# Groups of 512 nodes, more rows copied by hand and evictions on VectorE in a relational graph convolution

## The chip, the cores and the metric

The kernel runs on one core of a Trainium2 chip. The metric is the device time of one execution in microseconds. TensorE (PE) multiplies matrices, VectorE (DVE) and ScalarE (ACT) work element by element, GpSimd (POOL) issues the gathers here, and SyncE (SP) issues DMAs. ScalarE can issue DMAs as well, and does.

## The reference

Two layers of a relational graph convolution, then a residual and a layer norm. There are 50,000 nodes of 128 features, 850,000 edges sorted by target, 50,000 of them self loops, and 16 relations whose weights are mixtures of 8 bases.

```python
def _rgcn_layer(h, src, dst, rel, basis, w_comp, loop_w, bias):
    W = jnp.einsum('rb,bio->rio', w_comp, basis)
    seg = dst.astype(jnp.int32) * N_REL + rel.astype(jnp.int32)
    agg = jax.ops.segment_sum(h[src], seg, num_segments=N_ENT * N_REL)
    agg = agg.reshape(N_ENT, N_REL, -1)
    msg = jnp.einsum('nri,rio->no', agg, W)
    out = msg + h @ loop_w + bias
    return jax.nn.relu(out)
...
h = _rgcn_layer(entity_emb, src, dst, rel_type, basis1, w_comp1, loop_w1, bias1)
h = _rgcn_layer(h, src, dst, rel_type, basis2, w_comp2, loop_w2, bias2)
...
x = _layernorm(x + _L0_gnn_ref(x, ...), axis=-1)
```

## The kernel before

**Edges.** The first part of the program reads the edge list in ten blocks (`runs`), takes the 50,000 self loops out, and lays the other 800,000 edges out again (`FULL`, read back by `rows_of`). They make 6,250 tiles of 128 edges; ten tiles are a chunk, so a layer has C = 625 chunks. For each edge there is its source (`src`), the place of its target within a window of WN = 12 nodes (`key`) and its relation. This preparation is spread over the first chunks of layer 1, one step of the generator `coming` for each chunk.

**A chunk.** For each of its ten tiles the 128 source rows of 512 bytes are brought into a buffer `g` (L202, one indirect DMA of GpSimd for each tile). PE multiplies the tile with `hot`, which holds for each edge its weight for each of 8 bases, put at one of 12 places (L971): out comes, for one tile, a 128x96 sum in a PSUM tile `pa` that holds five tiles. Two evictions a chunk take `pa` to `aT` (ScalarE, L979). Two chunks later `slots` multiplies `aT` with the 8 bases (L734) into 120 slots, which ScalarE copies to SBUF (L739), and three chunks later `nodes_of` moves the slots to 128 nodes with masks (`masks_of`, L753; the product at L761). The nodes' own part, self loop and bias are added (L764) and the result is stored. In layer 2, the residual and the layer norm come before the store (`normed_steps`).

**The nodes' own part.** `from_itself` takes 128 nodes at a time: a load, a transpose, two products with four bases each (L710), their weighting on VectorE (L713), the loop product and bias (L722, L723), a sum over bases (L726) and a store to a DRAM tensor `L` (L727). `loaded` reads `L` back at the base node of each chunk, an offset that SyncE loads into a register. Neighbouring chunks' windows of 128 nodes overlap.

**Who brings the rows.** GpSimd gathers two chunks ahead (FETCH), into GATHERS = 5 buffers; the first gather of a chunk waits for the last product that read its buffer, by a dependency added by hand. From chunk 9 on, the last tile of every eighth chunk is not gathered: `row_by_row` has SyncE copy its 128 rows by 128 DMAs, each with an offset loaded from DRAM, and ScalarE does so for another of every eight chunks.

```python
HANDS = ((nc.sync, BY_HAND - 1), (nc.scalar, BY_HAND // 2 - 1))
def by_hand(c):
    return BY_HAND < c < C and ks(c) == K and any(c % BY_HAND == at for _, at in HANDS)
```

The DMAs of one such tile are spread over the eight chunks before its use, between the other instructions of their engine. Offsets are loaded 16 at a time (L798) and the rows are issued at L808.

**Order.** PE, GpSimd, VectorE and ScalarE run in the order in which the program states the work; `beside` puts a step of the own part, of `slots` or of the node part behind each of the ten products. All DMAs that SyncE and ScalarE issue take one of eight semaphores in turn, in the program's order, and each waits until the one before it on the same semaphore has landed.

Of the kernel before, what the change touches and what calls it, by code (L numbers as in the profile page):

```python
# [39 lines left out]
F32 = mybir.dt.float32  # L40
I32 = mybir.dt.int32
# [21 lines left out]
AHEAD = 4  # L63
# [8 lines left out]
BASES = 8  # L72
BY_HAND = 8
# [8 lines left out]
def tile_rgcn_resnorm(  # L82
# [21 lines left out]
    NG, NT = -(-R // P), -(-N // P)  # L104
# [9 lines left out]
    assert D == P and N >= P and edges.shape[0] == 1 and AT * NR == P and PER * NB * WN <= BANK and AT * PER * NB == WEIGHTS and PER == HALF and S <= P and C >= 4 and M > 0 and RUN - LK // 2 == LIVE and 2 * C <= NG * P and N <= 1 << 16 and E % ROW == 0  # L114
# [10 lines left out]
    ROW_AT = dram.tile([2 * C, P], I32, name="ROW_AT")  # L125
    NL = -(-(N + LK) // P) * P
    LREL = dram.tile([2 * NL, 1], I32, name="LREL")

    L = [dram.tile([N, D], F32, name=f"L{n}") for n in range(2)]
# [67 lines left out]
    ps_o = ctx.enter_context(tc.tile_pool(name="ps_o", bufs=1, space=PSUM))  # L197
    ps_n = ctx.enter_context(tc.tile_pool(name="ps_n", bufs=1, space=PSUM))
    ps_h = ctx.enter_context(tc.tile_pool(name="ps_h", bufs=2, space=PSUM))
# [6 lines left out]
    def turned(h, m, sb):  # L206

        tp = ps_o.tile([P, D], F32, name="po")
        nc.tensor.transpose(tp[:, :m], h, ident[:m, :m])  # L209
        hT = sb.tile([P, P], F32, name="hT")  # L210
        nc.scalar.copy(hT[:, :m], tp[:, :m])  # L211
        return hT[:, :m]
# [8 lines left out]
    key = consts.tile([P, 2 * C * HALF], BF16, name="key")  # L221


    base_i = consts.tile([1, C], I32, name="base_i")
    slot = consts.tile([P, C], F32, name="slot")
    next_slot = consts.tile([P, C], F32, name="next_slot")
    last_slot = consts.tile([P, 1], F32, name="last_slot")
    first_of = consts.tile([1, C], F32, name="first_of")
    base1 = consts.tile([1, C], F32, name="base1")
    minus = consts.tile([1, S], F32, name="minus")  # L230
# [4 lines left out]
    picked = consts.tile([P, 5 * NG + len(ROWS) + 4], F32, name="picked")  # L235
    ones = consts.tile([P, max(LIVE, C)], F32, name="ones")
# [10 lines left out]
    nc.vector.memset(minus, -1.0)  # L247
# [5 lines left out]
    def set_up(pool):  # L253
# [14 lines left out]
        po = ps_o.tile([P, D], F32, name="po")  # L268
# [146 lines left out]
    def loops_of(g, pool, m, d_i, k_f, r_i, loop, loops, asked):  # L415
# [15 lines left out]

        nc.vector.tensor_scalar(picked[0:1, 5 * g + 4 : 5 * g + 5], d_i[0:1, 0:1], float(asked()), None, op0=OP.is_ge)
        yield
# [8 lines left out]
    def rows_of(j, pool):  # L442
# [3 lines left out]
        parts = pool.tile([P, 2, LIVE, 2], F32, name="parts")  # L446
        for h in range(2):
            nc.sync.dma_start(
                parts[:m, h],
                FULL[h * NP + r0 * LIVE : h * NP + (r0 + m) * LIVE].rearrange("(p e) w -> p e w", e=LIVE),  # L450
            )
        if j:
            yield
        srcf = pool.tile([P, LIVE], F32, name="srcf")
        nc.vector.tensor_tensor(srcf[:m], parts[:m, 0, :, 0], parts[:m, 1, :, 0], op=OP.add)
        node = pool.tile([P, LIVE], I32, name="node")
        nc.vector.tensor_tensor(node[:m], parts[:m, 0, :, 1], parts[:m, 1, :, 1], op=OP.add)
# [20 lines left out]
        row_at = pool.tile([P, LIVE], F32, name="real").bitcast(I32)[:, :P]  # L478
        nc.vector.tensor_scalar(row_at[:m], srcf[:m, LIVE - P :], float(N - 1), float(4 * D), op0=OP.min, op1=OP.mult)
        nc.sync.dma_start(ROW_AT[r0 : r0 + m], row_at[:m])  # L480

# [3 lines left out]
        keyf = pool.tile([P, LIVE], F32, name="keyf")  # L485
# [6 lines left out]
        if (r0 + m) * LIVE > M:  # L492
# [6 lines left out]
                beyond[:m], place[:m, :LIVE], last[:m], 64.0, op0=OP.subtract, op1=OP.mult  # L499
# [8 lines left out]
        po = ps_o.tile([P, D], F32, name="po")  # L508
# [6 lines left out]
        nc.vector.tensor_scalar(base1[:, c0 : c0 + cs], half[0:1, :, 0], float(N - P), None, op0=OP.min)  # L515
        nc.vector.tensor_scalar(base_i[:, c0 : c0 + cs], base1[:, c0 : c0 + cs], float(4 * D), None, op0=OP.mult)

        a, b = max(c0 - 1, 0), c0 + cs - 1
        off = pool.tile([1, P], F32, name="off")
        nc.vector.tensor_tensor(off[:, : b - a], base1[:, a + 1 : b + 1], base1[:, a:b], op=OP.subtract)  # L520
        yield
        po = ps_o.tile([P, D], F32, name="po")
        for h in range(2):
            nc.tensor.matmul(po[:S, :cs], spread[h], half[:, :, h], start=h == 0, stop=False)
        nc.tensor.matmul(po[:S, :cs], minus, base1[:, c0 : c0 + cs], start=False, stop=True)
        nc.vector.tensor_scalar(slot[:S, c0 : c0 + cs], po[:S, :cs], within[:S], None, op0=OP.add)
        yield
        po = ps_o.tile([P, D], F32, name="po")
        nc.tensor.matmul(po[:, : b - a], ones[0:1, :P], off[:, : b - a], start=True, stop=True)
        nc.vector.tensor_tensor(next_slot[:S, a:b], slot[:S, a:b], po[:S, : b - a], op=OP.subtract)  # L530
        if b == C - 1:
            nc.vector.tensor_tensor(
                last_slot[:S], next_slot[:S, b - 2 : b - 1], po[:S, b - a - 1 : b - a], op=OP.subtract
            )
# [6 lines left out]
            ones[:m, :LIVE],  # L541
# [6 lines left out]
    def count_up(pool):  # L548
        last = 5 * NG + len(ROWS)
        off = pool.tile([1, C], F32, name="off_all")  # L550

        nc.vector.memset(off, float(N - 1))
        nc.vector.tensor_copy(off[:, : C - 1], first_of[:, 1:])
        nc.vector.tensor_tensor(off, off, base1, op=OP.subtract)
        nc.vector.scalar_tensor_tensor(
            off, off, float(P - 1), ones[0:1, :C], op0=OP.is_le, op1=OP.mult, accum_out=picked[0:1, last : last + 1]
        )

        in_time = pool.tile([1, C], F32, name="in_time")
        nc.gpsimd.iota(  # L560
            in_time,
            pattern=[[P * NT // C, C]],
            base=P * AHEAD - P,
# [3 lines left out]
        nc.vector.tensor_tensor(off, base1, in_time, op=OP.subtract)  # L567
        nc.vector.scalar_tensor_tensor(
            off, off, 0.0, ones[0:1, :C], op0=OP.is_le, op1=OP.mult, accum_out=picked[0:1, last + 1 : last + 2]
        )  # L570

        nc.vector.tensor_tensor(off[:, : C - 3], base1[:, 2 : C - 1], first_of[:, 1 : C - 2], op=OP.subtract)
        nc.vector.tensor_tensor(off[:, C - 3 : C - 2], base1[:, C - 1 :], first_of[:, C - 3 : C - 2], op=OP.subtract)
        nc.vector.scalar_tensor_tensor(
            off[:, : C - 2],
            off[:, : C - 2],
            1.0,
            ones[0:1, : C - 2],
            op0=OP.is_ge,
            op1=OP.mult,  # L580
            accum_out=picked[0:1, last + 3 : last + 4],
        )
        nc.vector.tensor_scalar(picked[0:1, last + 2 : last + 3], first_of[:, 0:1], 0.0, None, op0=OP.is_equal)
# [3 lines left out]
        total = ps_o.tile([P, D], F32, name="po")  # L587
# [4 lines left out]
            off[:, 1:2], total[:1, 1:2], float(E + 2 * NG * (P + 1) + 3 * C - 1), None, op0=OP.not_equal  # L592
# [3 lines left out]
    def normed(t, m, sb):  # L596

        *_, o = normed_steps(t, m, sb)
        return o

    def normed_steps(t, m, sb):
        st = sb.tile([P, 6], F32, name="st")
        nc.vector.bn_stats(st[:m], t)  # L603
        mv = sb.tile([P, 2], F32, name="mv")
        nc.vector.bn_aggr(mv[:m], st[:m])  # L605
        sd = sb.tile([P, 1], F32, name="sd")
        nc.scalar.activation(sd[:m], mv[:m, 1:2], AF.Sqrt, bias=eps[:m])  # L607
        yield
        rs = sb.tile([P, 1], F32, name="rs")
        nc.vector.reciprocal(rs[:m], sd[:m])  # L610
        nm = sb.tile([P, 1], F32, name="nm")
        nc.vector.scalar_tensor_tensor(nm[:m], mv[:m, 0:1], -1.0, rs[:m], op0=OP.mult, op1=OP.mult)  # L612
        o = sb.tile([P, D], F32, name="o")
        nc.scalar.activation(o[:m], t, AF.Identity, bias=nm[:m], scale=rs[:m])  # L614
        yield o

    def chunked():
        with (
# [8 lines left out]
            def at(c):  # L627

                if c % BASES == 0:
                    _, starts[:] = nc.values_load_multi_w_load_instructions(  # L630
                        base_i[0:1, c : min(C, c + BASES)],
                        engines=[mybir.EngineType.SP],
                        min_val=0,
                        max_val=(N - P) * 4 * D,
                        skip_runtime_bounds_check_because="bases are clamped to N - P, and no node is below 0",
                    )
                return starts[c % BASES]

            def nodes_at(of, start):
                return of.bitcast(U8).rearrange("n d -> (n d)")[ds(start, P * 4 * D)].rearrange("(p d) -> p d", p=P)  # L640

            def weights(c, n):
# [14 lines left out]
                for j in range(PER):  # L657
# [6 lines left out]
                    )  # L664
                yield pm.rearrange("e (t b) -> e t b", b=NB)

            def loop_weights(i, n):

                m = min(AT, NT - i) * NR
                rel = hp.tile([P, 2, P], I32, name="lrel")  # L670
# [544 lines left out]
```

## Time and profile before

| | before |
|---|---|
| median of 10 runs | 15,407.47 us (15,404.69 to 15,415.10) |
| the profiled execution, time | 15,413.04 us |
| its span | 15,411.3 us |
| granted TensorE clock in it | 0.805 |
| busy: PE, DVE, ACT, POOL | 11,650.9, 6,792.2, 2,523.9, 11,586.3 us |
| gathers (L202) | 2 x 6,096 |
| rows copied by hand (L808), each of SyncE and ScalarE | 2 x 9,856 |
| share of the 16 DMA engines, software and hardware queues | 18.7%, 9.0% |

The page gives busy time for each engine, with instructions that only issue a DMA or wait left out, so that SyncE has no line and a queue of DMAs on ScalarE does not count as busy. The groups give for each line the number of instructions, their mean duration in ns and the idle time of the engine just before them with what ended it; "issue" stands for idle time in which nothing was waited for. In a timeline the first column is the start in us, the second the time that the merged instructions took, and what stands in brackets is the idle time before them.

### The profile page before, as it was taken

How to read it: one execution, taken by the hardware profiler on the slowest of the kernel's cores; microseconds unless marked ns; L12 is line 12 of the kernel's file. 1: busy time of each engine (PE TensorE's matmuls, PEld its weight loads, DVE VectorE, ACT ScalarE, POOL GpSimd, SP SyncE). 2: the span in 40 equal slices, each digit the busy share in tenths (PEclk: the TensorE clock that was granted, in tenths of full speed). 3: DMA queues.
4: the chain of work that ended last, by engine and by line, in shares of the span. 5: the costliest groups of instructions: out<-in, count | busy, mean ns of one | idle time of the engine just before them, and what ended most of it. 6: DMA issues, size and time to landing. Idle time of an engine off the chain costs nothing. (4 is left out here: it accounts for less than half of the span.)

```text
span 15411.3 us, 255870 instructions
## 1 busy us (share of the span) xinstructions
PE 11650.9 (76%) x59202; PEld 9222.6 (60%) x59202; DVE 6792.2 (44%) x14585; ACT 2523.9 (16%) x6567; POOL 11586.3 (75%) x12224
## 2 busy tenths in 40 slices
PE   5777777776777777777777777777777777777777
PEld 4656666655565665556566565656666666655556
DVE  6544544445333333333344444444444444444444
ACT  1111111111111111111111111111111111111111
POOL 6777777777777777777777777777777777777777
PEclk8787787777788788888878888787777788788887
DMA  3222222222222222222222222222222222222222
GB/s 95 83 86 86 83 85 85 81 85 80 81 75 75 75 75 75 75 74 75 74 76 80 80 80 80 80 81 80 80 81 80 81 80 80 81 79 81 80 80 75
DMA packets 1236470, 1232.33 MB, mean 80 GB/s; under 512 B 318004, under 2 KB 1028332, under 8 KB 1234940
## 3 DMA queue, kind: packets, MB, share of 16 engines
q0 software_dynamic: 393696, 806.61, 18.7%
q1 hardware_dynamic: 798604, 397.62, 9.0%
q10 hardware_dynamic: 42640, 11.62, 0.3%
q8 instruction: 481, 7.88, 0.2%
q14 instruction: 1049, 8.59, 0.2%
HBM read 1059.71 MB, written 154.87 MB: 79 GB/s over the span
## 5 line engine op out<-in xcount | busy, mean ns | idle before, releaser
L971 PE MATMUL pa<-hot,g 128*128 128x96 f32 x24384 | 5953.0, 337 | 3302.8 <-DMA g<-H,src 1592.5
L971 PEld LDWEIGHTS pa<-hot,g 128*128 128x128 f32 x24384 | 4606.1, 234 | 5681.6 <-DMA g<-H,src 2233.8
L202 POOL DMA_INDIRECT g<-in_x_dram,src x6096 | 5794.4, 951 | 1890.2 <-issue 1764.5
L202 POOL DMA_INDIRECT g<-H,src x6096 | 5766.2, 946 | 1876.6 <-issue 1792.2
L734 PE MATMUL ps<-basis,aT 128*120 128x128 f32 x20000 | 3990.8, 334 | 0.0
L734 PEld LDWEIGHTS ps<-basis,aT 128*120 128x120 f32 x20000 | 3386.2, 237 | 0.0
L979 ACT COPY aT<-pa 128x480 f32<-128x480 f32 x2500 | 1397.9, 559 | 8246.9 <-DMA by_hand<-in_x_dram 3002.0
L713 DVE TENSOR_TENSOR by<-hb,lw 128x512 f32<-128x512 f32 x1564 | 1077.6, 689 | 3697.9 <-PE hb L710 3687.3
L710 PE MATMUL hb<-basis,hT 128*128 128x512 f32 x3128 | 2120.2, 767 | 4.2 <-ACT hT L211 4.2
L726 DVE TENSOR_REDUCE ls<-by 128x128 f32<-128x1152 f32 (+1 forms) x782 | 1657.0, 2119 | 13.5
L871 DVE TENSOR_TENSOR hot<-fixed,own 128x960 f32<-128x960 f32 x1250 | 1446.8, 1157 | 62.5 <-DVE own L864 1.8
L723 DVE TENSOR_TENSOR by<-po,bias 128x128 f32<-128x128 f32 (+1 forms) x782 | 227.6, 291 | 2267.9 <-PE po L722 2236.4
L761 PE MATMUL pn<-slots,own 120*128 120x128 f32 x5000 | 967.0, 325 | 32.9 <-DVE a L764 28.4
L864 DVE TENSOR_TENSOR own<-fixed,key 128x120 f32<-128x120 f32 x1250 | 343.1, 274 | 1139.2 <-PE fixed L658 1136.3
L761 PEld LDWEIGHTS pn<-slots,own 120*128 120x128 f32 x5000 | 813.0, 231 | 36.0 <-DVE a L764 30.5
L710 PEld LDWEIGHTS hb<-basis,hT 128*128 128x128 f32 x3128 | 601.8, 239 | 7.6 <-ACT hT L211 7.6
L607 ACT ACTIVATE sd<-mv,eps 128x1 f32<-128x1 f32 x625 | 184.2, 295 | 2375.6 <-DMA by_hand<-H 1871.7
L658 PE MATMUL fixed<-each,is_rel 128*128 128x64 f32 x3140 | 515.9, 326 | 3.9 <-DVE is_rel L653 3.9
L658 PEld LDWEIGHTS fixed<-each,is_rel 128*128 128x128 f32 x3140 | 497.6, 244 | 4.6 <-DVE is_rel L653 4.3
L209 PE MATMUL po<-ident,h_own 128*128 128x128 f32 (+1 forms) x782 | 271.9, 348 | 278.4 <-ACT lw L689 224.5
L614 ACT ACTIVATE o<-a,nm,rs 128x128 f32<-128x128 f32 x625 | 308.2, 493 | 960.8 <-DMA by_hand<-H 494.2
L753 DVE TENSOR_SCALAR own<-col,slot 120x128 f32<-120x128 f32 x1250 | 422.6, 338 | 0.0
(152 smaller groups left out, 4294.0 us busy)
## 6 DMA issues: line engine op xcount, KB each, us to landing
by_hand<-in_x_dram ACTq DMA_DIRECT2D x9856, 0.5 KB
by_hand<-in_x_dram SPq DMA_DIRECT2D x9856, 0.5 KB
by_hand<-H ACTq DMA_DIRECT2D x9856, 0.5 KB
by_hand<-H SPq DMA_DIRECT2D x9856, 0.5 KB
g<-in_x_dram,src POOLq DMA_INDIRECT x6096
g<-H,src POOLq DMA_INDIRECT x6096
ls_of<-L SPq DMA_DIRECT2D x1250, 64.0 KB
L<-ls SPq DMA_DIRECT2D x780, 64.0 KB
```

What stands on the lines that cost most here:

```text
L202: return nc.gpsimd.indirect_dma_start(out=to, out_offset=None, in_=of, in_offset=bass.IndirectOffsetOnAxis(ap=idx, axis=0))
L658: nc.tensor.matmul(of[:, :, j * NB : (j + 1) * NB], is_rel[:m, j * P : (j + 1) * P], EACH[n][:m], start=True, stop=True,)
L710: nc.tensor.matmul(hb[:m], hT, BASIS[n][:, b : b + few, :].rearrange("p b d -> p (b d)"), start=True, stop=True)
L713: nc.vector.tensor_tensor(by[:m, b : b + few, :], hb[:m].rearrange("p (b d) -> p b d", d=D), lw[:m, b : b + few, None].to_broadcast([m, fe ...
L726: nc.vector.tensor_reduce(ls[:m], by[:m].rearrange("p b d -> p d b"), AX.X, OP.add)
L734: nc.tensor.matmul(ps[: k * WN], aT[:, b, : k * WN], BASIS[n][:, b, :], start=b == 0, stop=b == NB - 1)
L753: nc.vector.tensor_scalar(own[:k], col[:k], at_node[:k], None, op0=OP.is_equal)
L761: nc.tensor.matmul(pn, own, st[i][: ks(i) * WN], start=j == 0, stop=j == len(masks) - 1)
L864: nc.vector.tensor_tensor(own[:, : ks(c)], grid[:, None, :].to_broadcast([P, ks(c), WN]), key[:, c * K : c * K + ks(c), None].to_broadcast ...
L871: nc.vector.tensor_tensor(hot[:, : ks(c)], pm[:, c % Q * K : c % Q * K + ks(c), :, None].to_broadcast([P, ks(c), NB, WN]), own[:, : ks(c), ...
L971: product = nc.tensor.matmul(pa[:, i * NB * WN : (i + 1) * NB * WN], g[:, k + i, :] if k + i < ks(c) - by_hand(c) else handed.pop(c), hot[ ...
L979: nc.scalar.copy(aT[:, :, k * WN : (k + m) * WN].rearrange("d b (i w) -> d i b w", w=WN), pa[:, : m * NB * WN].rearrange("d (i b w) -> d i ...
```

## The change

- Nodes are treated in groups of J x 128 = 512, four nodes to a partition. The 98 groups of a layer are summed in PSUM over all chunks that can touch them (`first(g)` to `final(g)`, 10 or 11 chunks); the slots are spread to four columns by `which` and moved by one product 128x512 for each chunk and group. The loop product is added to the same PSUM tile. `L` in DRAM, its store and its reading back at an offset are gone; the own part stays in SBUF. The nodes' result, norm and store go by 512.
- The evictions of `pa` go from ScalarE to VectorE; the copy of the slots becomes a VectorE product with `which`.
- SyncE and ScalarE copy a tile in every fifth chunk each, from chunk 6 on, spread over five chunks; offsets are loaded 32 at a time.
- The dependency by hand is gone: each gather waits for the product that read its own tile of the buffer.
- PSUM: one bank for `slots`, two for the groups' sums, two shared by the transposes and the own part.

```diff
-BASES = 8
-BY_HAND = 8
+J = 4
+NEAR = 128
+SP_EVERY = 5
+ACT_EVERY = 5
+OFFSETS = 32
...
-    ps_o = ctx.enter_context(tc.tile_pool(name="ps_o", bufs=1, space=PSUM))
-    ps_n = ctx.enter_context(tc.tile_pool(name="ps_n", bufs=1, space=PSUM))
-    ps_h = ctx.enter_context(tc.tile_pool(name="ps_h", bufs=2, space=PSUM))
+    ps_o = ctx.enter_context(tc.tile_pool(name="ps_o", bufs=2, space=PSUM))
+    ps_s = ctx.enter_context(tc.tile_pool(name="ps_s", bufs=1, space=PSUM))
+    ps_n = ctx.enter_context(tc.tile_pool(name="ps_n", bufs=2, space=PSUM))
...
+            def first(g):
+                return max(0, -(-(g * GN - NEAR) // (N // C)) - 1)
+            def final(g):
+                return min(C - 1, ((g + 1) * GN - 1 + NEAR) // (N // C))
...
             def slots(c, k, aT, n):
...
-                st = sb.tile([P, D], F32, name="slots", bufs=5)
-                nc.scalar.copy(st[: k * WN], ps[: k * WN])
+                st = sb.tile([P, J, D], F32, name="slots")
+                nc.vector.tensor_tensor(
+                    st[: k * WN],
+                    ps[: k * WN, None, :D].to_broadcast([k * WN, J, D]),
+                    which[: k * WN, c, :, None].to_broadcast([k * WN, J, D]),
+                    op=OP.mult,
+                )
...
-                    nc.tensor.matmul(pn, own, st[i][: ks(i) * WN], start=j == 0, stop=j == len(masks) - 1)
+                    nc.tensor.matmul(
+                        sums[g],
+                        own,
+                        of[:k].rearrange("s j d -> s (j d)"),
+                        start=c == first(g),
+                        stop=c == final(g),
+                    )
+                    if c == first(g):
+                        hT = hTs.pop(g)
+                        for j in range(J):
+                            nc.tensor.matmul(
+                                sums[g][:m, j * D : (j + 1) * D], hT[:, j, :m], LOOP[n], start=False, stop=False
+                            )
...
-            HANDS = ((nc.sync, BY_HAND - 1), (nc.scalar, BY_HAND // 2 - 1))
+            HANDS = ((nc.sync, SP_EVERY, SP_EVERY - 1), (nc.scalar, ACT_EVERY, ACT_EVERY // 2 - 1))
             def by_hand(c):
-                return BY_HAND < c < C and ks(c) == K and any(c % BY_HAND == at for _, at in HANDS)
+                if ks(c) < K:
+                    return []
+                return [i for i, (_, every, at) in enumerate(HANDS) if c > every and c % every == at]
...
+                steps = every * (K - 1)
+                for step in range(steps):
+                    for e in range(step * P // steps, (step + 1) * P // steps):
+                        if e % OFFSETS == 0:
+                            with tc.issue_after(behind[i]) if i in behind else ExitStack():
+                                _, offsets = nc.values_load_multi_w_load_instructions(
+                                    row_at[:, e : e + OFFSETS],
...
+                        row = to.bitcast(U8)[e : e + 1, :]
+                        behind[i] = engine.dma_start(row, byte[None, ds(offsets[e % OFFSETS], 4 * D)]).ins
...
-                        for k in range(ks(to) - by_hand(to)):
-                            fetched = gather(rows[buffer][:, k, :], of, src[:, to * K + k : to * K + k + 1])
-                            if k == 0 and buffer in read_by:
-                                tc.add_manual_dep(
-                                    fetched.ins,
-                                    read_by[buffer].name,
-                                    mybir.DependencyInfo(mybir.DependencyClass.Sync, mybir.DependencyReason.DATA),
-                                    reason="the whole buffer is read",
-                                )
+                        for k in range(ks(to) - len(by_hand(to))):
+                            gather(rows[buffer][:, k, :], of, src[:, to * K + k : to * K + k + 1])
...
-                                nc.scalar.copy(
+                                nc.vector.tensor_copy(
                                     aT[:, :, k * WN : (k + m) * WN].rearrange("d b (i w) -> d i b w", w=WN),
                                     pa[:, : m * NB * WN].rearrange("d (i b w) -> d i b w", i=m, w=WN),
                                 )
```

## The prediction

> **What bounds the kernel now.** I read the page's part 1 first, then the groups of POOL, then POOL's timeline in the middle of the span, then who waits for whom, and last the timeline of the two queues that copy rows by hand.
>
> ```profile
> PE 11650.9 (76%) x59202; PEld 9222.6 (60%) x59202; DVE 6792.2 (44%) x14585; ACT 2523.9 (16%) x6567; POOL 11586.3 (75%) x12224
> ...
> L202 POOL DMA_INDIRECT g<-in_x_dram,src x6096 | 5794.4, 951 | 1890.2 <-issue 1764.5
> L202 POOL DMA_INDIRECT g<-H,src x6096 | 5766.2, 946 | 1876.6 <-issue 1792.2
> ```
>
> PE and POOL look equally busy, and neither looks full. But POOL's idle time is almost all "issue": it waits for nothing.
>
> ```profile
> 7000.74 0.94 POOL L202 DMA_INDIRECT g<-in_x_dram,src  x1 [0.31 <-issue]
> 7001.98 0.94 POOL L202 DMA_INDIRECT g<-in_x_dram,src  x1 [0.30 <-issue]
> 7003.23 0.94 POOL L202 DMA_INDIRECT g<-in_x_dram,src  x1 [0.31 <-issue]
> ...
> 3691.64 0.94 POOL L202 DMA_INDIRECT g<-in_x_dram,src  x1 [17.14 <-DMA FULL<-full,to_i]
> ```
>
> 0.94 us of work and 0.30 us of gap make one gather each 1.25 us, and 12,192 x 1.25 = 15,240 us of a span of 15,411. The rest is a start of about 45 us, a 17 us wait in the first layer (last line above), another of 17 us between the layers, some 20 us after the last gather, and gathers that take longer while the edges are still being prepared. So the gathers set the time, and PE follows them:
>
> ```profile
> PEld pa L971 <- DMA g<-H,src: 2233.8, 3125, 2.4
> ACT aT L979 <- DMA by_hand<-in_x_dram: 3002.0, 689, 28.8
> SPq L808 <- DMA by_hand<-in_x_dram: 438.2, 1004, 5.3
> ```
>
> PE waits for gathers that have just landed. The two lines on by_hand say that ACT's and SP's queues are held by their own row copies; this matters below.
>
> **Fewer gathers.** A layer has 6,250 tiles. Before, 154 are copied by hand, so 6,096 are gathered. After, SyncE has chunks 9, 14, ... 624 and ScalarE 6, 11, ... 621: 124 each, and 6,002 are gathered. Over two layers 188 gathers go, at 1.25 us: **-235 us**, as long as POOL stays the bound. Five chunks then last 48 x 1.25 = 60.0 us; before, 48.8 x 1.25 = 61.0.
>
> **A wait on each gather.** Instead of the first gather of a chunk, every gather waits for PE. In 33 successive gathers of the timeline, three chunks, all gaps are 0.30 to 0.32 us, though about every tenth already carries that wait. Ends: nothing, or 0.01 us x 10,800 = 108 us. I take 0, the row that repeats. No gain either: POOL's list has no wait for PE worth naming.
>
> **Evictions and slots on VectorE.** 2,500 copies 128x480 leave ACT (1,398 us). On DVE the nearest rows are 128x512 from PSUM at 689 and 708 ns (L713, L472), the far end is ACT's 559: 1,400 to 1,770 us. The slots, 1,250 copies of 271 ns on ACT, become a 120x512 product at about 689 ns: 861 us. Away go the bias add (228 us), four in ten of 1,028 us of node work (512 nodes per instruction where it was 128 overlapping ones: about -600) and 434 masks of 0.32 us (-140). DVE goes from 6,792 to about 8,300 us, 55%; in the first quarter of the span, where it is 5 to 6 tenths busy now, to 8 tenths. What hides it: pa has two buffers, so an eviction is needed only five products (6 us) later, and DVE's longest instruction is 2.12 us. Were that gone, PE would be late by the rest, and POOL would feel it only after the five gather buffers, four chunks or 48 us. I take 0.
>
> The Trainium skill speaks against this move: "SBUF — State Buffer", section "Who interferes with whom", says that a VectorE copy in a two-port mode holds the port pair with which GpSimd writes its DMA descriptors. The row first: 2,498 masks (L753, SBUF to SBUF) run beside the gathers, and the gathers' means are 951 and 946 ns where an undisturbed one takes 0.94, at most 104 us in all. By "VectorE: DVE Perf Modes", section "Why PSUM operands drop a tier", an operand in PSUM keeps an instruction out of that mode, and pa is in PSUM; were the lock to hold for them, 2,500 x 0.69 us would be as much as 1.7 ms.
>
> **PE.** The slot products change from 2,500 of 128x128 (967 us) to 2,064 of 128x512. Priced by hb (two records, 767 ns each): 3,170 us; by the pair that took 1.05 us in one place of the timeline 2,170, by one that took 1.97 elsewhere 4,070. PE's busy time goes from 11.65 to between 12.9 and 14.8 ms, nearest 13.9, of 15.2: full to nine tenths, still under POOL. The granted clock is 0.805 now; PE would bind near 0.73. I take 0.
>
> **The stores between.** L is no longer stored and read back, and H1, out, x and h move 512 nodes at a time: SyncE's other DMAs fall from some 5,500 to 1,270. At 0.38 us each (timeline) this frees 1.6 ms of its queue. It is spent at once on the next step.
>
> **Rows by hand.** Each queue now issues 31,744 rows instead of 19,712, 128 in 60 us instead of 98. The price of a row:
>
> ```profile
> 7010.06 6.02 SPq L808 DMA_DIRECT2D by_hand<-in_x_dram  x16
> 7010.65 2.94 ACTq L808 DMA_DIRECT2D by_hand<-in_x_dram  x7
> 7018.79 4.87 SPq L808 DMA_DIRECT2D by_hand<-in_x_dram  x14
> ...
> L798 SPq TENSOR_LOAD <-row_at x1232: 971/1170/3624, 158.3 to 15342.7; - x176
> ```
>
> That is 0.376, 0.42 and 0.348 us. 128 rows take 44.5 to 53.8 us. Offsets are loaded 32 at a time, four loads a tile: 1.17 us as for 16, or at most double: 4.7 to 9.4. SyncE has 5.6 other DMAs in five chunks: 2.1. Sum 51 to 65 us per tile, against 60.0. There is a second way to sum it. In the program's order a row waits for the landing of the eighth row DMA before it, whichever queue that was on. In the changed order about half of the rows alternate between the queues, and half stand in runs of about 17 rows of one queue, while the other waits. For 32 rows of each: 15 pairs at 0.376 (5.6 us) and two runs of 17 at 0.348 (11.8). At each end of a run eight rows overlap (2.8 us) less one landing, which is at most the 1.5 us of four alternating rows: 1.3 us back for each run. 14.8 us, times four 59 us; without any overlap 70, with runs that cost the other queue nothing 53. I take 59 us, nearest to the row with both queues at work (0.376): just under the supply, so the gathers still bind. This is the weakest number of the sum: over 60 us, each further us costs 248 us in the kernel.
>
> **Start, layers, end.** The last group of a layer has wider steps behind its last gather (slots 0.69 for 0.27, sums 1 to 2 us for 0.6 to 1.3, the node work four times as wide): +3 us between the layers, +5 at the end.
>
> **Sum.** The profiled execution took 15,413.0 us (span 15,411.3). 15,413 - 235 + 8 = 15,186, and 5.6 less for the median of the runs (15,407.5): 15,180. Queues that are 98% full will now and then be late beyond the buffers; I allow 20 us: **15,200 us**. Of a difference under 0.2% (31 us) a measurement of this kernel could not say that it is one.
>
> **Rivals.**
> *The copying queues bind (slower).* Place: SyncE's and ScalarE's rows; mechanism: runs of one queue hold the other, and loads of 32 offsets come on top. Against POOL's 60.0 us, a tile of 62 us gives 15,200 + 2 x 248 = 15,700, of 63 us 15,940; it is slower than before from 61.0 us on. For it: sums of 51 to 70 us straddle the point, and ACT already waits 3,002 us for row copies in layer 1. Against it: that waiting comes with evictions queued between the rows, which leave ACT; and 5,500 DMAs of SyncE become 1,270. Another page of the skill would favour it: "DMA: Bandwidth & Descriptors", section "Issuing engines are not separate DMA queues", says that all queues share the same 16 DMA engines, so that more issuers only save issue time. Here issue time is the bound, and the DMA engines are 2 tenths busy, so that rule does not decide.
> *The same queues only just full:* a tile of 60.3 to 61 us, 15,270 to 15,440, a small gain or none.
> *PE binds:* a clock of 0.70 or less with 13.9 ms x 0.805 of work gives 15,980. Against it: the clock is granted while PE works, and PE will idle less.
> *The change doesn't do what it says:* the gathers' period grows by 0.02 us from the new waits or from DVE; 12,004 x 0.02 = 240 us, and the time stays at 15,420.
>
> **How the numbers follow.** Gathers bind: 0.60, with 15,150 (no leak, all end effects zero, slow gathers of the preparation fewer) to 15,270. Queues just full: 0.07, of which 0.04 still faster. Queues bind and slower: 0.26, about half of it under 15,800. PE: 0.03. Period grows: 0.04, half the same, half slower. Faster 0.64, same 0.05, slower 0.31. The range from 15,150 to 15,800 leaves out the far half of the slower case, PE and a little below: under 0.2.
>
> **What would show it.** Right: 6,002 gathers a layer, still with 0.30 us gaps from "issue", and POOL idle for nothing else. Wrong: gaps of POOL that PE ends, PE waiting on by_hand tiles, and SPq or ACTq waiting for row copies over more than a few per cent of the span (queues bind); gather means above 951 ns or gaps above 0.31 (period grows); PE over 95% busy (PE binds).

## The result: 12% slower, and the profile after

The changed kernel takes **17,311.75 us** (median of 8 runs, 17,300.8 to 17,322.86) against 15,407.65 of the kernel before (28 runs): a ratio of **1.1236**, 95% interval 1.1226 to 1.1246. Forecast were 15,200 us, in a range that ended at 15,800. The first rival, copying queues that bind, happened, and far beyond the price given to it.

The page after, parts 1, 4 and 5:

```profile
span 17296.6 us, 293484 instructions
...
PE 10433.1 (60%) x58712; PEld 8077.4 (47%) x58712; DVE 8182.2 (47%) x14006; ACT 421.3 (2%) x896; POOL 11403.7 (66%) x12037
...
DMA 9%; SPq 5%; ACTq 4%; issue 3%; DVE 1%; PE 1%; ACT 0%; DVEq 0%
...
L204 POOL DMA_INDIRECT g<-H,src x6002 | 5682.0, 947 | 2881.8 <-PE pa L972 1396.8
L204 POOL DMA_INDIRECT g<-in_x_dram,src x6002 | 5695.9, 949 | 2573.3 <-PE pa L972 1085.5
```

No engine is three quarters busy any more. A gather costs what it did (947 and 949 ns), but POOL's largest stop is now a wait for PE. 12,004 gaps of 0.305 us would be 3,660 us; there are 5,455. The chain, which could be followed back only over the last 23% of the span, names the row copies: their transfers, SyncE's queue (SPq), ScalarE's queue (ACTq). hT is the transposed tile of a group's own nodes, copied from PSUM by ScalarE (L699) and multiplied on PE at L710; by_hand is a tile of copied rows.

Who waits for whom (total us, times, longest):

```profile
ACT hT L699 <- DMA by_hand<-in_x_dram: 3790.4, 88, 67.1
ACT hT L699 <- DMA by_hand<-H: 3550.2, 92, 58.4
...
PE po L710 <- ACT hT L699: 2994.8, 188, 41.8
...
POOL g L204 <- PE pa L972: 2482.4, 2700, 19.6
```

and the same for SyncE's own queue:

```profile
SPq L836 <- DMA by_hand<-in_x_dram: 1527.4, 2824, 9.1
SPq L836 <- DMA by_hand<-H: 1456.9, 2868, 7.9
...
SPq L798 <- ACT ls L595: 51.3, 41, 4.2
```

Read from the bottom up: rows wait for rows (2,984 us of SyncE's time, 17% of the span), the hT copies stand in ScalarE's queue behind rows, PE waits for hT, and the gathers wait for PE's products. The last line is SyncE's largest wait for another engine. Of the whole span SyncE's queue waits 197 us for other engines and ScalarE's, counted in the same way, about 190: something over 1%, so the two queues are full. The two queues in the middle of the second layer:

```profile
10022.45 24.00 SPq L836 DMA_DIRECT2D by_hand<-H  x51
10046.55 0.22 SPq L819 DMA_DIRECT2D row_at<-ROW_AT  x1
10046.87 25.83 SPq L836 DMA_DIRECT2D by_hand<-H  x51
```

```profile
10007.80 37.84 ACTq L836 DMA_DIRECT2D by_hand<-H  x70
10045.68 0.27 ACT L678 COPY lw<-po 128x128 f32<-128x128 f32 x1 [37.42 <-DMA by_hand<-H]
10049.82 9.25 ACTq L836 DMA_DIRECT2D by_hand<-H  x26
10059.16 0.59 ACT L699 COPY hT<-po 128x512 f32<-128x512 f32 x1 [13.21 <-DMA by_hand<-H]
```

They hardly rest. 51 rows take 24 to 26 us with their loads of offsets: about half a microsecond a row, where the kernel before showed 0.35 to 0.42 in its bursts, without loads. 250 spells of five chunks (two layers of 625 chunks) in 17,297 us are 69.2 us each; the supply was 60.0.

### The profile page after: what moved, and what is told of

It reads as the page before. It is cut to its first block, busy times and chain, and to the rows that moved or that the text cites. A ratio compares the mean times of both kernels' runs of the same rounds, so it can differ in the third digit from the quotient of the medians.

```text
span 17296.6 us, 293484 instructions
## 1 busy us (share of the span) xinstructions
PE 10433.1 (60%) x58712; PEld 8077.4 (47%) x58712; DVE 8182.2 (47%) x14006; ACT 421.3 (2%) x896; POOL 11403.7 (66%) x12037
## 5 line engine op out<-in xcount | busy, mean ns | idle before, releaser
L972 PEld LDWEIGHTS pa<-hot,g 128*128 128x128 f32 x24008 | 3923.1, 211 | 2078.5 <-issue 1273.2
L972 PE MATMUL pa<-hot,g 128*128 128x96 f32 x24008 | 4278.3, 287 | 693.4 <-DVE aT L980 531.3
L710 PE MATMUL po<-basis,hT 128*128 128x512 f32 x3136 | 1982.4, 719 | 3350.5 <-ACT hT L699 2994.8
L732 PE MATMUL ps<-basis,aT 128*120 128x128 f32 x20000 | 3339.1, 293 | 1.8 <-DVE slots L737 1.8
L980 DVE COPY aT<-pa 128x480 f32<-128x480 f32 x2500 | 1626.8, 651 | 3314.6 <-PE pa L972 3291.9
L732 PEld LDWEIGHTS ps<-basis,aT 128*120 128x120 f32 x20000 | 2751.9, 197 | 12.0 <-DVE slots L737 2.2
L768 PE MATMUL pn<-slots,own 120*128 120x512 f32 x4128 | 2363.8, 692 | 500.7 <-DVE own L751 495.6
L717 DVE TENSOR_TENSOR by<-po,lw 128x512 f32<-128x512 f32 x1568 | 1063.4, 685 | 2612.2 <-PE po L710 2592.9
L710 PEld LDWEIGHTS po<-basis,hT 128*128 128x128 f32 x3136 | 547.7, 219 | 3402.4 <-ACT hT L699 3025.9
L737 DVE TENSOR_TENSOR slots<-ps,which 120x512 f32<-120x512 f32 x1250 | 849.3, 679 | 14.2 <-PE ps L732 13.5
```

What stands on the lines that cost most here:

```text
L710: nc.tensor.matmul(hb[:m], hT[:, j, :m], BASIS[n][:, b : b + few, :].rearrange("p b d -> p (b d)"), start=True, stop=True,)
L717: nc.vector.tensor_tensor(by[:m, b : b + few, :], hb[:m].rearrange("p (b d) -> p b d", d=D), lw[:m, j, g % T, b : b + few, None].to_broadc ...
L732: nc.tensor.matmul(ps[: k * WN, :D], aT[:, b, : k * WN], BASIS[n][:, b, :], start=b == 0, stop=b == NB - 1)
L737: nc.vector.tensor_tensor(st[: k * WN], ps[: k * WN, None, :D].to_broadcast([k * WN, J, D]), which[: k * WN, c, :, None].to_broadcast([k * ...
L768: nc.tensor.matmul(sums[g], own, of[:k].rearrange("s j d -> s (j d)"), start=c == first(g), stop=c == final(g),)
L972: nc.tensor.matmul(pa[:, i * NB * WN : (i + 1) * NB * WN], others.get(k + i, g[:, k + i, :]), hot[:, k + i].rearrange("e b w -> e (b w)"), ...
```

## The experiments

Theory Q: the two copying queues bind. The expectations call it A or the queue theory; in A1 the queues hold each other by the order of their rows, in A2 a row costs 0.54 us in any order. Rival B: groups of 512 nodes, evictions on VectorE, or a wait on each gather lengthen the chain. On two chips the kernel before took 20,873 and 20,885 us, so that of the runs every8, sync5, aligned5, before5 and every6, made there, only ratios are told. Where there is a repeat elsewhere they lie 0.6 to 9% below it, so the readings rest on the other runs, among them the repeats, whose names end in _n. The two kernels, run again: after_again 17,316.46 us (ratio 1.1221, 1.1189 to 1.1254), before_again 15,433.33. Their expectations were for a slower chip and fall away, since both ran where the kernel before takes 15,432; they repeat the first result.

> The changed kernel as it is, run where the other experiments ran: there the kernel before takes 20,880 us instead of 15,407, so the experiments need their own base. Theory A (the copying queues bind, and the chip there slows all engines' streams alike): between 1.04 (aligned tiles) and 1.2 of before, 22,000 to 25,000 us, with 0.12 of the 15,407 us scale as the middle: about 23,400. Theory B (groups, evictions or gather waits cost the time): it stands well above the variant with tiles in every eighth chunk only by what the 188 rarer gathers save, so below 19,500.

> The kernel before as it is, for its trace where the other experiments ran: 20,850 to 20,930 us. If engines' instruction streams are what is slower there, PE and the two copying queues show idle time that nothing releases (issue) of 3 to 5 ms on PE, where the first profile had 1.1, and GpSimd's gathers still take 0.94 us.

**All of the change except the number of rows: every8, every8_n.** The tiles go back to every eighth chunk, 6,096 gathers a layer as before.

```diff
-SP_EVERY = 5
-ACT_EVERY = 5
+SP_EVERY = 8
+ACT_EVERY = 8
```

> The changed kernel with SyncE and ScalarE copying a tile in every eighth chunk, as before, instead of every fifth; 2 x 6,096 gathers as before. Theory A (the two queues of row copies bind: 69 us for a tile of 128 rows where five chunks of gathers take 60): eight chunks take 97.5 us, the queues are 7 tenths full, the gathers bind again and the time is 15,380 to 15,450 us, POOL's gaps 0.30 us, PE not waiting for hT. Theory B (the groups of 512, the evictions on VectorE or the wait on each gather cost the time): it stays above 16,500.

> Every eighth chunk again, where the kernel before takes 15,400 us. Theory A (the copying queues bind): the gathers bind, 2 x 6,096 at 1.25 us, 15,380 to 15,450 us, POOL's gaps 0.30 us. Theory B (groups of 512, evictions on VectorE or the wait on each gather cost the time): above 16,500.

Measured: 15,418.95 us, ratio 1.0005 (0.9996 to 1.0015); every8 on a slower chip 0.9102 (0.9086 to 0.9117). Of every8_n the page, part 1, POOL's groups, and SyncE's waits for rows:

```profile
PE 12125.2 (79%) x58712; PEld 8608.8 (56%) x58712; DVE 8249.4 (54%) x14006; ACT 422.0 (3%) x896; POOL 11585.1 (75%) x12225
```

```profile
L204 POOL DMA_INDIRECT g<-in_x_dram,src x6096 | 5792.0, 950 | 1889.7 <-issue 900.9 <-PE pa L972 309.4 <-PE ps L732 288.0
L204 POOL DMA_INDIRECT g<-H,src x6096 | 5767.1, 946 | 1880.6 <-issue 890.7 <-PE ps L732 333.1 <-PE pa L972 317.0
```

```profile
SPq L836 <- DMA by_hand<-in_x_dram: 2394.6, 1977, 22.2
SPq L836 <- DMA by_hand<-H: 2362.5, 2132, 21.2
```

The same gathers, the same means, the same idle time before them (3,770 us; 3,767 before). PE and VectorE now end some of the gaps, but no gap is longer for it. So groups, evictions and the waits of the gathers cost nothing that can be seen, and B falls: the loss comes with the greater number of rows. It is also why nothing was won here: with as many gathers the time is that of before. One thing warns: SyncE's rows wait longer for earlier rows here, 4,757 us, than in the changed kernel, 2,984. With shared semaphores a queue also waits for rows while the other queue stands elsewhere. What marks the queues as full is that they wait for nothing else: for other engines SyncE's queue waits 1,175 us here and ScalarE's some 4,560, against 197 and about 190 in the changed kernel.

**One queue alone: sync5, sync5_n.** SyncE still copies a tile in every fifth chunk, ScalarE none; 6,126 gathers a layer.

```diff
-            HANDS = ((nc.sync, SP_EVERY, SP_EVERY - 1), (nc.scalar, ACT_EVERY, ACT_EVERY // 2 - 1))
+            HANDS = ((nc.sync, SP_EVERY, SP_EVERY - 1),)
```

> The changed kernel with SyncE alone copying a tile in every fifth chunk and ScalarE none; 2 x 6,126 gathers. Theory A1 (the queues hold each other, since each DMA waits for the eighth one before it in the common order, and single rows in between runs of the other queue lose time): alone, a tile costs 128 x 0.325 + 4 loads x 2.13 + about 2.3 us of other DMAs = 52 us against 61, gathers bind, 15,450 to 15,530 us. Theory A2 (a row costs 0.54 us on its queue whoever else issues): the tile still takes 69 us and the time stays near 17,300.

> SyncE alone, a tile in every fifth chunk, again where the kernel before takes 15,400 us. Theory A1 (the two queues hold each other): 52 us for a tile against 61, gathers bind, 15,450 to 15,530 us. Theory A2 (a row costs 0.54 us on its queue whoever else issues): 17,300.

Measured: 15,493.79 us, ratio 1.0054 (1.0034 to 1.0074); sync5 0.9997 (0.9984 to 1.0009). The number of gathers alone makes 15,408 + 60 x 1.25 = 15,483. POOL's first group and SyncE's timeline in sync5_n:

```profile
L204 POOL DMA_INDIRECT g<-in_x_dram,src x6126 | 5816.3, 949 | 1899.2 <-issue 863.6 <-PE pa L972 321.4 <-DMA g<-in_x_dram,src 307.3
```

```profile
10002.40 40.56 SPq L836 DMA_DIRECT2D by_hand<-H  x103
10043.06 0.23 SPq L819 DMA_DIRECT2D row_at<-ROW_AT  x1
10072.83 0.38 SPq L798 DMA_DIRECT2D out_dram<-ls  x1
```

103 rows in 40.6 us, loads included, then 30 us in which it copies no row. The same queue with the same rows keeps up when the other one is silent; the two hold each other up. On the slower chip that was different: there a row of sync5 came on average 0.57 us after the one before it (0.335 in sync5_n), a tile took 20,919 / 250 = 83.7 us, and SyncE's queue waited only some 240 us for other engines, so that one queue alone was full. Why a row costs more there is open.

**The order of the rows: aligned5, aligned5_n.** In the changed kernel the program alternates the queues' rows for a while and then has runs of about 17 of one queue; 14,151 of SyncE's 31,744 rows stand in runs of eight or more. With both tiles in the same chunks it is 1,349.

```diff
-            HANDS = ((nc.sync, SP_EVERY, SP_EVERY - 1), (nc.scalar, ACT_EVERY, ACT_EVERY // 2 - 1))
+            HANDS = ((nc.sync, SP_EVERY, SP_EVERY - 1), (nc.scalar, ACT_EVERY, ACT_EVERY - 1))
```

> The changed kernel with ScalarE's tile in the same chunks as SyncE's (c % 5 == 4 for both), so that both load their 32 offsets at the same time; the same 2 x 6,002 gathers and the same number of rows. In the program's order 14,151 of SyncE's 31,744 rows stood in runs of 8 or more, now 1,349. Theory A1 (runs of one queue hold the other): a stretch of 32 rows takes 32 x 0.376 to 0.41 + 2.2 us, a tile 60 to 64 us, the time 15,200 to 16,000 us. Theory A2 (a row costs 0.54 us in any order): 17,300. Theory B (groups, evictions, gather waits): 17,300.

> Tiles of both queues in the same chunks, so that both load offsets together, again where the kernel before takes 15,400 us. SyncE's rows in runs of 8 or more: 1,349 of 31,744 instead of 14,151. Theory A1 (runs of one queue hold the other): a tile 60 to 64 us, 15,200 to 16,000 us. Theory A2 (a row costs 0.54 us in any order) and theory B: 17,300.

Measured: 16,949.70 us, ratio 1.0998 (1.098 to 1.1017); aligned5 1.0435 (1.0418 to 1.0453). A miss: setting the two queues' rows and loads side by side takes away 362 us of the 1,904, not all of it. SyncE's queue in aligned5_n:

```profile
SPq L836 <- DMA by_hand<-in_x_dram: 1207.8, 3696, 16.4
SPq L836 <- DMA by_hand<-H: 1181.8, 3612, 17.2
```

Rows that stand nearly all in turn still wait 2,390 us for earlier ones, in more waits than after, of 0.33 us on average for 0.52.

**Smaller loads: offs16.**

```diff
-OFFSETS = 32
+OFFSETS = 16
```

> The changed kernel with offsets loaded 16 at a time, as before, instead of 32. Rows in runs of 8 or more fall from 14,151 to 8,397 for SyncE, and a run is as long as eight rows, which the eight semaphores cover; loads cost 8 x 1.2 us a tile instead of 4 x 2.1. Theory A1: faster than the changed kernel, a tile 61 to 66 us, 15,400 to 16,500 us. Theory A2 or B: within 1% of 17,312.

Measured: 17,042.82 us, ratio 1.1059 (1.1037 to 1.1081), 1.6% under the changed kernel; a miss too. Lines on the loads (ns: shortest, median, longest), of after:

```profile
L828 ACTq TENSOR_LOAD <-row_at x992: 2117/2242/4457, 49.5 to 17220.0; - x199
L828 SPq TENSOR_LOAD <-row_at x992: 2027/2129/4392, 53.2 to 17258.1; - x199
```

A load of 32 offsets, from the tile row_at in SBUF, takes 2.13 and 2.24 us; one of 16 takes 1.17 and 1.30 in the kernel before. With 16 in a load, SyncE's loads take 10.1 us a tile instead of 8.6, while the idle time before its rows falls from 18.8 us to 15.6; with some 0.8 us more elsewhere, about 1 us a tile is left over.

**The old kernel with more rows: before5.** Groups, evictions and waits as before, rows in every fifth chunk and 32 offsets to a load.

```diff
-BY_HAND = 8
+BY_HAND = 5
+OFFSETS = 32
```

> The kernel before with one part of the change alone: a tile in every fifth chunk from SyncE and from ScalarE, offsets loaded 32 at a time and spread over five chunks as after; groups, L in DRAM, evictions on ScalarE and one wait for each chunk as before. Theory A: the queues bind, and SyncE has some 17 DMAs more in five chunks than after, ScalarE its evictions: slower than the changed kernel, 17,300 to 19,500 us. Theory B: about 15,200.

Measured once, on a slower chip: 1.25 times the kernel before. On that chip one queue alone can be full (sync5), so it supports Q and does not show it: there, more rows and the larger loads are enough to lose, with nothing else of the change.

**Is the wait for hT a cause? ht_dve.**

```diff
-                nc.scalar.copy(hT[:, :, :m], po.rearrange("p (j e) -> p j e", j=J)[:, :, :m])
+                nc.vector.tensor_copy(hT[:, :, :m], po.rearrange("p (j e) -> p j e", j=J)[:, :, :m])
```

> The changed kernel with the 784 hT copies on VectorE instead of ScalarE, so that they no longer queue behind ScalarE's row copies. Queue theory (the two queues cannot deliver a tile of each in under 69 us, and the waits for hT are only where it shows): 17,100 to 17,400 us, PE's wait for hT goes and its wait for by_hand takes its place. Rival (the copies of hT queued behind row copies delay the products, and through them the gathers): 16,500 us or less.

Measured: 17,338.88 us, ratio 1.1254 (1.1236 to 1.1273): no change. (The trace has 196 hT copies, not the 784 of the expectation.) The waits in ht_dve:

```profile
ACT sd L587 <- DMA by_hand<-H: 5551.4, 86, 90.7
...
POOL g L204 <- PE pa L972: 2485.0, 2525, 28.3
...
PE po L710 <- DVE by L717: 967.8, 111, 47.7
...
PE po L710 <- DVE hT L699: 862.1, 78, 43.7
PE pa L972 <- DMA by_hand<-in_x_dram: 799.7, 81, 25.2
```

PE's wait for hT shrank from 2,995 to 862 us, others took its place, by_hand among them, and POOL's wait is the same to 3 us. The line of 2,995 us was where the lack showed, not its cause. ScalarE's other work (sd, the first line) still stands behind its rows, so this run clears the hT copies alone.

**Blocks of rows: blocks32.** As aligned5_n, with

```diff
-                    for e in range(step * P // steps, (step + 1) * P // steps):
+                    for e in range(step * P // steps // 32 * 32, (step + 1) * P // steps // 32 * 32):
```

> The changed kernel with both tiles in the same chunks, and each queue issues its rows in blocks of 32 instead of in turn with the other's; rows, loads and gathers are the same in number. Queue theory (a row waits for the landing of the eighth row before it in the program's order, whichever queue that was on): within a block of 32 the other queue can start only when the 25th row has landed, 8 x 0.325 less than the block: 24 x 0.325 + 1.5 = 9.3 us for 32 rows, 18.6 us for 32 rows of both, 74 us for a tile of each, loads hidden in the other's turn, and 3 us of other DMAs: 77 us, 248 times: 18,500 to 19,500 us. Rival (a row costs more with both queues at work because they share hardware, not because of the order): 16,950 as with rows in turn, or less, since the queues now work one after the other.

Measured: 17,318.78 us, ratio 1.1245 (1.1226 to 1.1264). Neither case: in the order that was built the blocks are mostly taken apart again, and only some 5,200 of SyncE's rows stand in runs of eight or more. It says nothing on why a row is dear.

**Depth by itself: depth4, depth8.** In the program every row waits for the eighth row DMA before it, whichever queue that was on: one queue alone has eight rows in flight, two queues in turn have four each. The semaphores in the traces agree: in aligned5_n 28,300 of SyncE's 31,744 rows take the next semaphore but one after the DMA before them, in sync5_n every row the next one. Here SyncE copies alone, as in sync5_n, and the depth is set by what a row overwrites.

```diff
+                nc.vector.memset(to, 0.0)
...
-                        row = to.bitcast(U8)[e : e + 1, :]
+                        row = to.bitcast(U8)[e % 4 * 32 : e % 4 * 32 + 1, :]
```

(in depth8 `e % 8 * 16`)

> As sync5_n (SyncE alone copies a tile in every fifth chunk), but every row is written over the fourth row before it, so that it waits for that row's landing: four rows in flight on one queue, with no other queue at work. This leaves out most of the copied rows (four of 128 are kept, a clearing of the tile on VectorE comes on top); their number, size and loads are the same. Queue theory (with both queues at work each has only four of its rows in flight, and a row then costs a quarter of a landing): row to row 0.41 to 0.44 us as in aligned5_n, 54 + 9 + 1.4 + 2.6 = 67 us for a tile against 49 x 1.25 = 61.2 us of supply: 248 x 67 + 100 = 16,700, 16,400 to 16,900 us. Rival (a row costs more with both queues at work because of hardware that they share): row to row 0.334, 15,450 to 15,550 us.

> The control of depth4: every row is written over the eighth row before it (eight of 128 are kept), which is the row that it waits for in sync5_n too. Both theories: row to row 0.334 us, 15,450 to 15,550 us. If the writing over of rows, the few partitions written or the clearing cost something by themselves, it shows here.

depth8: 15,494.95 us, ratio 1.0056 (1.0039 to 1.0073), as expected and within about 1 us of sync5_n. depth4: 19,077.73 us, ratio 1.2379 (1.2359 to 1.24), a miss by over 2,000 us. Its rows tell the price of the depth all the same. From the starts of the rows in the traces (mean from one row to the next on a queue with nothing else between; median from issue to landing):

| kernel | queues | row to row, SyncE / ScalarE, us | landing, us |
|---|---|---|---|
| sync5_n | SyncE | 0.335 | 1.41 |
| depth8 | SyncE | 0.334 | 1.41 |
| depth4 | SyncE | 0.378 | 1.29 |
| aligned5_n | both | 0.426 / 0.435 | 1.62 |
| after | both | 0.400 / 0.412 | 1.53 |

Four in flight instead of eight costs 0.044 us a row with no second queue at work. The rest, up to 0.426, goes with the longer landing: four rows to one mean landing plus 0.12 us, the 0.12 chosen to fit depth4, gives (1.39 + 0.12) / 4 = 0.378 there and (1.65 + 0.12) / 4 = 0.44 in aligned5_n. By this estimate each of the two theories has about half: depth 5.6 us of 128 rows, landing 6.1. The rows of after are a little cheaper, since a run of one queue goes at 0.325 while the other stands still; it pays for that after its loads.

Why depth4 is so slow otherwise, from the waits of SyncE's queue and of all engines in it:

```profile
SPq L685 <- PE pa L973: 995.6, 148, 18.0
SPq L623 <- DVE own L751: 861.8, 184, 18.8
```

```profile
PE pa L973 <- DMA by_hand<-H: 4337.6, 124, 42.7
PE pa L973 <- DMA by_hand<-in_x_dram: 4155.6, 124, 59.3
```

PE waits for every one of the 248 tiles, 34 us each, and the queue that should bring it stands 17 us a tile waiting for VectorE, PE and ScalarE, mostly before its other DMAs, where sync5_n stood 8. That the two waits feed each other is argued, not shown; what starts them in this order of the program was not tried.

**A version that beats both: every6, every6_n, aligned6.** A tile for each queue in every sixth chunk; in aligned6 both in the same one.

```diff
-SP_EVERY = 5
-ACT_EVERY = 5
+SP_EVERY = 6
+ACT_EVERY = 6
```

> The changed kernel with a tile in every sixth chunk from each queue; 2 x 6,044 gathers. Theory A (the copying queues bind, about 69 us for a tile): six chunks of gathers take 72.5 us, so the gathers bind again, with the queues 95% full: 15,270 to 15,450 us, 0.98 to 1.003 of before, POOL hardly waiting for PE. Theory B (groups, evictions or the wait on each gather cost the time): 16,500 or more, over 1.07 of before.

> The changed kernel with a tile in every sixth chunk for each queue, on a chip where the kernel before takes 15,410. Queue theory: 69 us of demand for a tile of each against 58 gathers x 1.25 = 72.5 us of supply, so the gathers bind again: 103 tiles of each queue in a layer, 6,044 gathers, 12,088 x 1.25 + 190 = 15,300, 15,250 to 15,450 us, faster than the kernel before by 0.5 to 1%. Rival (the queues at 95% are late often enough to hold the gathers): 15,500 to 16,000.

> As every6_n, but with both tiles in the same chunks, so that the rows of the queues stand in turn: 67.6 us of demand against 72.5. Queue theory: the gathers bind, the same 15,250 to 15,400 us, at or a little under every6_n. Rival: as there, 15,500 to 16,000.

Measured: every6_n **15,304.52 us**, ratio 0.9934 (0.9917 to 0.9951); aligned6 15,306.11, ratio 0.9935 (0.9918 to 0.9951); every6 0.9665 (0.9649 to 0.9681). POOL in every6_n:

```profile
L204 POOL DMA_INDIRECT g<-in_x_dram,src x6044 | 5742.9, 950 | 1875.1 <-DMA g<-in_x_dram,src 791.8 <-issue 561.2 <-PE pa L972 277.1
L204 POOL DMA_INDIRECT g<-H,src x6044 | 5722.0, 947 | 1864.6 <-DMA g<-H,src 815.8 <-issue 579.9 <-PE pa L972 237.2
```

3,740 us of gaps for 12,088 gathers: POOL sets the time again. 104 gathers fewer make 130 us by the 1.25, and 103 us come out: with their gaps the gathers take 123 us less than in the kernel before, and some 13 us more lie outside them. Here the order of the rows makes no difference, and about 69 us of demand stand against 72.5 of supply either way; SyncE's queue in every6_n waits 554 us for other engines, 2.7 us a tile, so it is nearly full.

## Why the prediction was wrong, point by point

**What failed: "Rows by hand", the 59 us.** The prediction called it its weakest number. SyncE's queue after, with means from the trace beside the prediction's terms:

| term, us a tile | prediction | measured |
|---|---|---|
| rows, one to the next | 44.5 to 53.8 | 122.4 x 0.400 = 49.0 |
| loads of 32 offsets, to the next row | 4.7 to 9.4, without waits | 4 x 3.52 = 14.1 |
| these two | second sum 59 | 63.1 |
| other DMAs and waits before them and before loads | 2.1, none in the 59 | 6.3 |
| sum | 51 to 65; taken 59 | 69.4 |

The rows of the table take in all the time from SyncE's first row to its last, 17,215 us for 248 tiles, so their sum is that time and not a second proof of it; that the queue is full is seen from the 197 us in which it waits for other engines.

Two mistakes, then. The second sum has no term for loads or other DMAs, and it was set against the supply as if it were the queue's whole time; with the first sum's own 4.7 and 2.1 it would have been 66 us and, at 248 us for each us over 60, some 16,700. Of the 10.4 us that are missing, 4.1 stand in rows and loads together and 6.3 in the other DMAs with their waits; these are 1,506 DMAs of SyncE, where the prediction counted 1,270. And a load was priced as its own duration. It takes 2.13 us, near the end that was named and not taken (twice 1.17), and it holds the other queue too: from the start of a load to the next row pass 3.52 us after, 2.41 in aligned5_n, 2.30 with one queue. aligned5_n divides in the same way: 52.2 + 9.6 + 6.1 = 68.0 us. The row's own 0.376 was nearly right, because of the runs at 0.325. The bound of 53 does not follow from the terms given (15 x 0.376 + 17 x 0.348, times four, is 46); nothing rested on it.

**The rival's arithmetic held to 1%.** From 60 us of supply, 69.2 us of demand by its 248 us each: 15,200 + 9.2 x 248 = 17,480; measured 17,312. What was too small was its size (62 to 63 us) and its chance, 0.26. The sum "without any overlap 70" stood in the text, and the range left it out.

**Fewer gathers, -235 us: its condition failed.** It held "as long as POOL stays the bound", and after, POOL no longer was. Where it is again, in every6_n, 104 gathers fewer bring 103 us, the gathers and their gaps themselves 123 us, about the price that was taken.

**A wait on each gather, 0 taken: right.** every8_n has 3,770 us of gaps, the kernel before 3,767.

**Evictions and slots on VectorE, 0 taken: right.** The copies take 651 ns (1,627 us; 1,400 to 1,770 said), the slots 679 ns (689 said), VectorE 8,182 us (8,300 said). In every8_n the gathers have means of 950 and 946 ns beside 2,500 evictions from PSUM by VectorE. The rule of the Trainium skill that the prediction weighed, "SBUF — State Buffer", section "Who interferes with whom", shows no price here; since all these evictions read PSUM, that is no test of it for copies within SBUF. VectorE's 8 tenths in the first quarter did not come: it is 5 to 7 tenths busy there in every8_n.

**PE, 0 taken: right.** 12.1 ms in every8_n at a clock of 0.863; if all of it went with the clock, 13.0 at 0.805, where 12.9 to 14.8 was said.

**The rule on issuers.** Rows on two queues move 2 tiles in 67.8 us, on one queue 1 in 54 (41.1 + 9.2 + 3.9 in sync5_n, its waits for other engines left out). The Trainium skill, "DMA: Bandwidth & Descriptors", section "Issuing engines are not separate DMA queues", says that more issuers only save the sequencer's time. That agrees as far as it goes: the second queue brings 1.6 times the rows, not twice, though the DMA engines are 2 tenths busy. What the queues share in these traces is the eight semaphores, and so the depth in flight; and a row lands later with both at work.

**The signs.** Of the three named signs of the losing case one tells it: gaps of POOL that PE ends, and by their length alone, up to 19.6 us. In every8_n PE ends 2,053 of them at L972 too, none over 0.3 us. Queues waiting for row copies came too, over 17% of the span, but every8_n, which does not lose, has 31%, so this sign marks no loss by itself. PE's wait on by_hand stayed small (230 us and 125): PE waited for hT instead, and in ht_dve, where it does so less, its wait on by_hand grows to 800 and 308.

**Still open:** why a landing takes 1.62 us with both queues and 1.41 with one; what starts the waits in depth4; and why rows cost more on the slower chips. The old kernel with more rows (before5) was measured on such a chip alone.

## What to carry to other kernels

A queue that issues many small DMAs is to be summed like an engine: rows, register loads and every other DMA, each with what it holds up on a neighbour, in one sum against the supply, and never two half sums side by side. To see whether such a queue is full, look at what it waits for besides its own kind of DMA. When completion slots are shared, a second queue in turn with the first halves its depth, so a price read from a short burst of one queue does not hold when both are always at work. If demand is 15% over supply, thin the work until it fits: here every sixth chunk in place of every fifth turned 12% of loss into 0.7% of gain.

## What the runs showed of the hardware that was not expected

A register load grows almost in proportion to its size: 1.17 us for 16 offsets on SyncE, 2.13 for 32, so about 0.06 us an offset and 0.2 fixed.

Rows written to the same eight partitions again and again land no later than rows spread over all 128: 1.41 us in depth8 and in sync5_n.

The granted clock went with how much PE worked, in kernels with nearly the same matmuls: 0.863 where PE was busy 79% (every8_n), 0.780 at 60% (after), 0.748 at 52% (depth4). It is not that alone: sync5 on the slower chip had 0.746 at 59%. PE's busy times cannot be compared between these runs without the clock.
